# Counts of neighbours as 61-row products issued behind the lookups, with other costs and allowances in the slot planner

## The chip, the cores and the metric

The kernel runs on one core of one Trainium2 chip. The metric is the device time of one execution in microseconds (us); a comparison of two kernels is made on the same chip. The engines of the core work side by side, each on its own queue in order: TensorE (PE in the profile, its weight loads PEld), VectorE (DVE), ScalarE (ACT), GpSimd (POOL) and SyncE (SP, which issues transfers here).

## The reference

Four graph layers run over 16 graphs of 1024 nodes with 128 features, each followed by a layer norm over `x + layer(x)`. Cut to what matters:

```python
# layer 0: attention over the neighbours
h = clip(scores * mask, 0, CLAMP_HI) - NEG_PENALTY * (1 - mask);  out = softmax(h) @ v
# layer 1: a maximum over the neighbours
pre = p[:, :, None, :] + q[:, None, :, :] + b
out = max over neighbours j of relu(pre) * adj
# layer 2: a sum over the neighbours, then two dense products with a relu between
# layer 3: each graph's adjacency is first thinned row by row ("dilation", 1024 steps in order),
#          then three convolutions with batch norms, and a dense product
```

Layer 1 is `relu(p[i] + max of q[j] over the neighbours j of i)`, for each of 128 features.

## The kernel before, in words

**Subsets instead of neighbours.** The maximum of layer 1 is not taken neighbour by neighbour. The 1024 candidates of a graph are cut into groups of 6 (`GS`), and two groups make a subset step of 12 candidates (`PS`). For each group a table holds, for all 64 subsets of its 6 members, the maximum of q over that subset. For each node the subset that its adjacency row picks is looked up by a product: a 0/1 column ("hot") with one 1 among the 64 rows times the table. A graph has 86 such steps (`NP`), 16 graphs have 1376, and each step is a *slot* of two halves of 512 nodes. In a half:

- `count` (L799, L800) makes the hot columns for the slot after next: a product of the signs in `lit` with ten steps' worth of columns of the adjacency (`AT`, 120 rows, fp8) gives for each of the 128 (2 x 64) subsets how many of its members agree, and ACT's relu with the column `one_less` as bias leaves 1 where all do and 0 elsewhere.
- `look_up` (L830) does four products of 64 rows and 512 columns: the high part of the table for the two groups, then the low part, added up in PSUM (`pg`, two buffers of two banks).
- DVE takes the maximum of `pg` and the running `best` (L890), 128 x 1024 elements.

Every second slot, `table` (L811, L814) turns the next two steps' tables by TensorE and ACT copies out the high part; `low_part` (L819, L821) half a slot later subtracts the high part and copies the low part. The count's `pm` and the table's `pt` share two PSUM banks (tag `subset`).

**What runs between.** Everything else of layers 0, 1 and 2 (of the graph after and the graph before) and layer 3's dilation is cut into small pieces that a planner puts into the halves while the program is written. Streams written as generators (`scores`, `attend`, `rest`, `tables_of`) ask for an engine at a stated cost (`ask("PE", 0.86, ...)`). In each half each engine gets half of its allowance per slot (`ROOM`), at most one whole allowance saved up; a stream goes on while its engine's allowance is above zero, and the cost is taken off. The costs are microseconds of the author's; they decide only in which half a piece stands, not what it does. `dilation` has due times of its own, counted in slots; `dilate_on` emits its next part when it is due, and takes its DVE cost off. The pieces of PE share two PSUM banks by turns (tag `shared`, `taken` and `given`).

**The order in a half**, as the planner writes it, is the order of each engine's queue (`manual_schedule`): the lookup; the pieces; `low_part` in the first half of odd slots; `count` for the slot after next; `table` in the second half of even slots; the maximum. So on PE a count stands behind the pieces of its half, and on ACT its relu behind theirs.

**Loads.** `load_columns` (L744 to L751) brings `AT` for ten slots with one transfer on POOL's queue, two chunks ahead, into four buffers; a graph has nine chunks, the last of which has 64 rows and is cleared first (L750). The adjacency is float32 in memory and is converted by the transfer.

Ahead of the slots the first graph's scores are made, 132 us in all; behind them come layer 3's convolutions (from 5167 us on), which the change does not touch.

Of the kernel before, what the change touches and what calls it, by code (L numbers as in the profile page):

```python
# [43 lines left out]
PS = 2 * GS  # L44
PC = 10
CH = PC * PS
NP = -(-N // PS)
TG = 12
R, G = 32, 4
# [11 lines left out]
def subset_tables():  # L61

    half = P // 2
    s = np.arange(half)
    lit = np.zeros((CH, PC, P), np.float32)
    for j in range(CH):
        a, k = divmod(j % PS, GS)
        lit[j, j // PS, a * half:(a + 1) * half] = np.where((s >> k) & 1, 1.0, -1.0)
    size = sum((s >> k) & 1 for k in range(GS))
    return lit, np.tile(1.0 - size, 2).astype(np.float32).reshape(P, 1)  # L70


@with_exitstack
def tile_graph_layers(ctx: ExitStack, tc, a, out):
# [27 lines left out]
    nc.vector.memset(ones_b, 1.0)  # L102
    mhalf = consts.tile([P, T], F32, name="mhalf")
    nc.vector.memset(mhalf, -0.5)
    lit = consts.tile([CH, PC, P], F8, name="lit")
    nc.gpsimd.dma_start(out=lit, in_=a["lit"])
    less = consts.tile([P, P], F32R, name="less")
    nc.vector.tensor_scalar_mul(less, ident, -1.0)
    one_less = consts.tile([P, 1], F32, name="one_less")
    nc.sync.dma_start(out=one_less, in_=a["one_less"])  # L110

    def weight(name, shape=(P, P), how=None, pool=consts):
        t = pool.tile(list(shape), F32, name="w_" + name)
# [124 lines left out]
    def layers_012():  # L238
# [50 lines left out]

        def product_of(lhsT, rhs, dst, func, bias, delay=0.5):  # L290
            for h, s in enumerate(halves):
                yield ask("PE", 0.86, take=True, delay=0.5 if h else delay)
                p = shared("pp")
                nc.tensor.matmul(p, lhsT, rhs[:, s], start=True, stop=True)
                yield ask("A", 0.6, give=True, same=True)
                if bias is None:
                    nc.scalar.copy(dst[:, s], p)  # L297
                else:
                    nc.scalar.activation(dst[:, s], p, func, bias=bias)

        def scores(b):

            if b > 1:
                yield ask("Pool", 0, after=("p", b - 1))
            if b > 2:
                yield ask("Pool", 0, after=("rest", b - 3))
            load_rows(b)
            xT = w4.tile([P, N], F32, name="xT")
            yield from columns_of(xT, X[b])
            qT = w4.tile([P, N], F32, name="qT")  # L310
            yield from product_of(WqT, xT, qT, AF.Relu, bq)
            kT = w4.tile([P, N], F32, name="kT")
            yield from product_of(WkT, xT, kT, AF.Relu, bk)
            v = values[b] = w4.tile([P, T, D], F32, name="v")
            for h in range(2):
                yield ask("PE", 1.1, take=True)
                pv = shared("pv").rearrange("p (t d) -> p t d", d=D)
                nc.tensor.matmul(pv, ones_b[:3, :], four(bv3), start=True, stop=False)
                for t in range(4):
                    nc.tensor.matmul(pv[:, t, :], xT[:, (4 * h + t) * P:(4 * h + t + 1) * P], WvT,  # L320
                                     start=False, stop=(t == 3))
                yield ask("A", 0.6, give=True, same=True)
                nc.scalar.activation(v[:, 4 * h:4 * h + 4, :], pv, AF.Relu)
            for t in range(T):

                yield ask("A", 1.05)
                off = w4.tile([P, N], BF, name="off", tag="pen")
                nc.scalar.activation(off, An[b][:, t, :], AF.Identity, bias=ones[:, 0:1], scale=-1.0)
                if t > 1:
                    yield ask("PE", 0, same=True, after=("back", b, t - 2))  # L330
                e = w4.tile([P, N], F32, name="e", bufs=2)

                tops = small.tile([P, 2], F32, name="tops")
                for h, s in enumerate(halves):
                    yield ask("PE", 1.07, take=True)
                    psc = shared("psc")
                    nc.tensor.matmul(psc, qT[:, t * P:(t + 1) * P], kT[:, s], start=True, stop=False)
                    nc.tensor.matmul(psc, penalty, off[:, s], start=False, stop=True)
                    yield ask("V", 0.66, give=True)
                    nc.vector.tensor_scalar(e[:, s], psc, CLAMP_HI, None, op0=ALU.min, op1=ALU.max,  # L340
                                            accum_out=tops[:, h:h + 1])
                yield ask("V", 0.1, same=True)
                top = small.tile([P, 1], F32, name="top")
                nc.vector.tensor_scalar(top, tops[:, 0:1], tops[:, 1:2], -1.0, op0=ALU.max, op1=ALU.mult)
                yield ask("A", 1.1)
                total = small.tile([P, 1], F32, name="total")
                nc.scalar.activation(e, e, AF.Exp, bias=top, accum_out=total)
                exps[b, t] = e, total
                happened["e", b, t] = now
            yield ask("A", 0.01, after=("X1", b), delay=0.5)  # L350
            xT = w4.tile([P, N], F32, name="xT1", tag="xT")
            yield from columns_of(xT, X[b])
            q = w4.tile([P, NP * PS], F32, name="q", bufs=2)
            nc.gpsimd.memset(q[:, N:], LOWEST)
            yield from product_of(W01[:, 1, :], xT, q[:, :N], None, None)
            qs[b] = q
            happened["q", b] = now
            if b > 1:
                yield ask("A", 0, same=True, after=("y1", b - 2))
            p = ps[b] = w4.tile([P, N], F32, name="p", bufs=2)  # L360
            yield from product_of(Wd, xT, p, AF.Identity, b01)
            happened["p", b] = now

        def attend(b):
            for t in range(T):
# [14 lines left out]
                for h in range(2):  # L380
# [2 lines left out]
                        pav = shared("pav")[:, :D]  # L383
                    for c in range(4 * h, 4 * h + 4):
                        nc.tensor.matmul(pav, eT[:, c, :], values[b][:, c, :], start=(c == 0), stop=(c == T - 1))  # L385
                yield ask("V", 0.4, give=True)
                share = small.tile([P, 1], F32, name="share")
                nc.vector.reciprocal(share, total)
                nc.vector.scalar_tensor_tensor(y[:, t, :], pav, share, X[b][:, t, :], op0=ALU.mult, op1=ALU.add)
# [354 lines left out]
        def load_columns(at):  # L744
            b, c = divmod(at, T + 1)
            if b < B:
                rows = min(CH, N - c * CH)
                t = AT[at] = apool.tile([CH, N], F8, name="AT", bufs=4)
                if rows < CH:
                    nc.gpsimd.memset(t, 0.0)  # L750
                nc.gpsimd.dma_start(out=t[:rows], in_=adjT[b, c * CH:c * CH + rows])  # L751

        An, AT, subs, qs, ps, values, exps, bests, hots, tables = ({} for _ in range(10))
        now, taken, given, held = 0, 0, {}, {}
        pending = {}

        ROOM = {"PE": 1.2, "A": 0.8, "V": 2.2, "Pool": 9.0}
        room = dict.fromkeys(ROOM, 0.0)  # L760

        def start(stream, first=False):
# [29 lines left out]
        def count(s, h):  # L792
# [3 lines left out]
            if h == 0:  # L796
                hots[s] = w2.tile([P, N], F32R, name="hot", bufs=3)
            pm = psum.tile([P, 512], F32, tag="subset", name="pm", bufs=2)
            nc.tensor.matmul(pm, lit[:, r, :], AT[b * (T + 1) + c][:, halves[h]], start=True, stop=True)  # L799
            nc.scalar.activation(hots[s][:, halves[h]], pm, AF.Relu, bias=one_less)  # L800

        def table(s):

            b, g = divmod(s, NP)
            g0 = g - g % TG
            assert ("sub", b, g0) in happened, (s, [(x.__name__, pending[x]) for x in streams], room)
            pt = psum.tile([P, 512], F32, tag="subset", name="pt", bufs=2)[:, :2 * P]
            if g + 2 - g0 == min(TG, NP - g0):
                happened["used", b, g0] = now
# [5 lines left out]
            tables[s] = pt, high  # L815

        def low_part(s):
            pt, high = tables[s]
            nc.tensor.matmul(pt, less, high, start=False, stop=True, skip_group_check=True)  # L819
            low = w2.tile([P, 2 * P], F32R, name="low", bufs=2)  # L820
# [21 lines left out]
        def dilate_on():  # L842
            nonlocal due, wants_bank
            if due <= now and not (wants_bank and taken >= 2 and given.get(taken - 2, 1e9) > now):
                after, cost, wants_bank = next(dilate, (B * NP, 0, False))
                due += after
                room["V"] -= cost

        def slot(s, last):
# [11 lines left out]
                if b:  # L861
                    start(rest(b - 1))
            if s >= 0 and g % PC == 0:
                load_columns(b * (T + 1) + g // PC + 2)
            for h in range(2):
                now = s + 0.5 * h
                for e in ROOM:
# [1 line left out]
                if s >= 0:  # L869
                    pg = psum.tile([P, 2, 512], F32, tag="wide", name="pg", bufs=2)  # L870
                    look_up(s, h, pg)
                early = s >= 0 and due < now
                if early:
                    dilate_on()
# [3 lines left out]
                    dilate_on()  # L878
                if h == 0 and s % 2 and s + 1 < last:
                    low_part(s + 1)  # L880
                if s + 2 < last:
                    count(s + 2, h)
                    if h and s % 2 == 0:
                        table(s + 2)
                if s >= 0:
                    own = bests[b][:, :, halves[h]]
                    if g == 0:
# [6 lines left out]
        dilate = dilation()  # L894
        due, wants_bank = 0.0, False
        load_x(0)
        for at in range(2):
            load_columns(at)
        front, back = scores(0), attend(0)
        for t in range(T):  # L900
            while ("e", 0, t) not in happened:
# [332 lines left out]
```

## Time and profile before

| | us |
|---|---|
| median of 3 runs | 6459.39 (6446.67 to 6460.74) |
| the profiled execution | 6458.95 |
| its span, first to last instruction | 6457.2 |
| first lookup to last lookup | 132 to 5167 |
| mean granted TensorE clock | 0.93 of full |

In the profile a line such as `L890 DVE TENSOR_TENSOR best<-best,pg 128x1024 ... x2720 | 3258.7, 1215 | 556.8 <-PE pg L830 546.8` gives a group of equal instructions: their line, engine, operation, output and inputs, shape and number, then their busy time in us and the mean of one in ns, then how long the engine was idle just before them and what ended most of that. A line of the waits gives who waited for whom, the sum in us, how many times, and the longest. PE's ends are modelled: two products that follow each other are best compared by their starts. In the names, `128*128` or `64*128` is the part of the array that a product uses, rows first.

### The profile page before, as it was taken

To read this page: it belongs to the slowest core of one execution; us is meant where nothing else is said; L and a number is where in the kernel's file an instruction comes from. 1 tells how busy PE (TensorE), PEld (TensorE's weight loads), DVE (VectorE), ACT (ScalarE), POOL (GpSimd) and SP (SyncE) were. 2 spreads that over 40 slices of the span, in tenths; PEclk is the share of its full clock that TensorE was granted. 3 is DMA by queue.
4 is the path that set the end of the run, shared out by engine and by line. 5 is a ranking of instruction groups with operands and counts; after the bars stand their busy time and mean duration, and the time that the engine had idled before them with its cause. 6 is when DMAs were issued, how large, how long until landed. Compare 5 with 4: busy or idle time off the path is not lost. (4 is left out here: it accounts for less than half of the span.)

```text
span 6457.2 us, 90620 instructions
## 1 busy us (share of the span) xinstructions
PE 5729.3 (89%) x29184; PEld 2962.2 (46%) x29354; DVE 4978.8 (77%) x7877; ACT 3946.3 (61%) x7142; POOL 3502.1 (54%) x11319
## 2 busy tenths in 40 slices
PE   6989999989899999999989998989998867877998
PEld 3444444444444444444444444444443335555654
DVE  3888888888888888888888888888888834444445
ACT  4667666666667666766666666666665623333755
POOL 2665766666666666766666666666666511110113
PEclk8989899999899999999999999998998988888999
DMA  5121212121212121212121212121211065654545
GB/s 38 13 30 21 35 21 36 21 34 21 34 21 37 20 35 20 34 20 32 24 34 20 34 20 34 20 35 20 35 21 18 20 101 106 126 103 111 206 167 186
DMA packets 478402, 317.32 MB, mean 49 GB/s; under 512 B 301162, under 2 KB 429668, under 8 KB 473828
## 3 DMA queue, kind: packets, MB, share of 16 engines
q0 software_dynamic: 105648, 84.20, 15.0%
q1 hardware_dynamic: 367600, 226.13, 11.9%
q8 instruction: 230, 3.77, 0.2%
q10 hardware_dynamic: 4676, 1.19, 0.1%
q14 instruction: 248, 2.03, 0.1%
HBM read 412.71 MB, written 117.18 MB: 82 GB/s over the span
## 5 line engine op out<-in xcount | busy, mean ns | idle before, releaser
L890 DVE TENSOR_TENSOR best<-best,pg 128x1024 f32<-128x1024 f32 x2720 | 3258.7, 1215 | 556.8 <-PE pg L830 546.8
L800 ACT ACTIVATE hot<-pm,one_less 128x512 fp32r<-128x512 f32 x2752 | 1882.7, 689 | 736.9 <-PE pm L799 727.5
L830 PE MATMUL pg<-hot,high 64*128 64x512 f32 x5504 | 1436.1, 519 | 239.2 <-DVE best L890 231.4
L830 PE MATMUL pg<-hot,low 64*128 64x512 f32 x5504 | 1139.8, 411 | 0.0
L799 PE MATMUL pm<-AT,lit 120*128 120x512 fp8e4 x2752 | 1110.3, 404 | 20.9 <-ACT hot L800 8.5
L830 PEld LDWEIGHTS pg<-hot,high 64*128 64x128 f32 x5504 | 533.6, 191 | 1018.9 <-DVE best L890 510.5
L830 PEld LDWEIGHTS pg<-hot,low 64*128 64x128 f32 x5504 | 553.0, 198 | 0.0
L658 POOL TENSOR_SCALAR sc<-low_counts,half_mask,rest 16x1 f32<-16x1 f32 x992 | 351.8, 355 | 323.7 <-DVE rest L644 218.8
L799 PEld LDWEIGHTS <-lit 120*128 120x128 fp8e4 x2752 | 272.6, 99 | 520.5 <-issue 460.2
L663 POOL TENSOR_SCALAR sc<-sc 16x1 f32<-16x1 f32 x992 | 397.3, 401 | 105.1
L821 ACT CAST low<-pt 128x256 fp32r<-128x256 f32 x688 | 256.1, 372 | 258.2 <-PE pt L819 255.0
L1039 POOL TENSOR_TENSOR length<-length,mhalf 128x8 f32<-128x8 f32 x48 | 78.9, 1644 | 570.8 <-DVE length L1038 570.8
L660 POOL TENSOR_SCALAR sc<-sc 16x1 f32<-16x1 f32 x992 | 315.0, 318 | 107.7
L819 PE MATMUL pt<-high,less 128*128 128x256 f32 x688 | 294.1, 427 | 85.0 <-ACT high L814 78.2
L703 POOL TENSOR_SCALAR shifts<-centre 128x4 f32<-128x4 f32 x32 | 10.5, 327 | 656.9 <-DVE width L699 633.6
L665 POOL TENSOR_SCALAR hit<-V,sc 16x31 bf16<-16x31 bf16 (+30 forms) x992 | 361.1, 364 | 0.0
L666 POOL TENSOR_SCALAR last_rank<-V,sc 16x31 f32<-16x31 bf16 (+30 forms) x992 | 344.5, 347 | 0.0
L996 ACT CAST m<-near 128x1024 fp32r<-128x1024 fp8e4 x256 | 253.4, 1044 | 112.6 <-DVE near L965 59.6
L475 DVE TENSOR_TENSOR sub<-sub,q 128x24 f32<-128x24 f32 (+11 forms) x768 | 303.3, 396 | 24.0 <-ACT q L297 10.4
L811 PE MATMUL pt<-ident,sub 128*128 128x128 f32 x1376 | 286.1, 291 | 26.7 <-ACT hot L800 22.3
L385 PE MATMUL pav<-v,eT 128*128 128x128 f32 x2048 | 301.7, 293 | 2.1 <-ACT eT L378 2.1
L1009 PE MATMUL pagg<-m,high 128*128 128x512 f32 x768 | 277.3, 432 | 13.2 <-ACT high L1002 13.2
(268 smaller groups left out, 9754.6 us busy)
## 6 DMA issues: line engine op xcount, KB each, us to landing
removed<-gone SPq DMA_DIRECT2D x128, 256.0 KB
An<-in_adj_dram POOLq DMA_DIRECT2D x16, 1024.0 KB, 14.8
E<-in_adj_dram POOLq DMA_DIRECT2D x128, 128.0 KB, 5.8
gone_all<-removed POOLq DMA_DIRECT2D x64, 256.0 KB, 12.3
near<-in_adjT_dram POOLq DMA_DIRECT2D x16, 1024.0 KB, 17.9
kept<-near SPq DMA_DIRECT2D x16, 1024.0 KB
share<-share SPq DMA_DIRECT2D x32, 512.0 KB
hidden<-r SPq DMA_DIRECT2D x32, 512.0 KB
```

Of the source, the lines that this page charges most:

```text
L385: nc.tensor.matmul(pav, eT[:, c, :], values[b][:, c, :], start=(c == 0), stop=(c == T - 1))
L475: nc.vector.tensor_max(sub[:, :n_g, n:2 * n], sub[:, :n_g, 0:n], qg[:, 2 * g0:2 * g0 + n_g, k:k + 1].to_broadcast([P, n_g, n]))
L658: gp.tensor_scalar(half, mine, half_mask[:, m], rest[:, n:n + 1], op0=ALU.mult, op1=ALU.add)
L660: gp.tensor_scalar(sf, half, 5.5, sf, op0=ALU.is_gt, op1=ALU.mult)
L663: gp.tensor_scalar(to, at, sf, none, op0=ALU.subtract, op1=ALU.subtract)
L665: gp.tensor_scalar(hit[:, n, n + 1:], V[:, n, n + 1:], at, None, op0=ALU.is_equal)
L666: gp.tensor_scalar(last[:, n + 1:], V[:, n, n + 1:], to, None, op0=ALU.is_le)
L799: nc.tensor.matmul(pm, lit[:, r, :], AT[b * (T + 1) + c][:, halves[h]], start=True, stop=True)
L800: nc.scalar.activation(hots[s][:, halves[h]], pm, AF.Relu, bias=one_less)
L819: nc.tensor.matmul(pt, less, high, start=False, stop=True, skip_group_check=True)
L830: nc.tensor.matmul(pg[:, a], part[rows, at * P:(at + 1) * P], hots[s][rows, halves[h]], start=(k == 0), stop=(k == 1))
L890: nc.vector.tensor_max(own, own, pg)
```

## The change

1. The signs `lit` are stored twice, on partitions 0 to 59 and 64 to 123, for five steps each, in bf16; a 61st row holds one minus the size of each subset, and a row of ones in `AT` meets it. A count is then a product of 61 rows, on the lower or the upper half of the array, and its relu has no bias column.
2. `AT` is two fixed bf16 buffers, set to one at the start. A chunk is loaded as two transfers of 60 rows, one chunk ahead.
3. In a half, `count` stands right behind the lookup, ahead of the pieces.
4. Some asked costs are higher, the tables and the dilation's products are charged to PE's allowance, and the allowances per slot are 1.6 (1.2) for PE and 1.5 (2.2) for DVE.

What is computed stays the same.

```diff
+SUB = CH // 2
...
-    lit = np.zeros((CH, PC, P), np.float32)
-    for j in range(CH):
+    lit = np.zeros((2, half, PC // 2, P), np.float32)
+    for j in range(SUB):
         a, k = divmod(j % PS, GS)
-        lit[j, j // PS, a * half:(a + 1) * half] = np.where((s >> k) & 1, 1.0, -1.0)
+        lit[:, j, j // PS, a * half:(a + 1) * half] = np.where((s >> k) & 1, 1.0, -1.0)
...
-    lit = consts.tile([CH, PC, P], F8, name="lit")
+    lit = consts.tile([P, PC // 2, P], BF, name="lit")
     nc.gpsimd.dma_start(out=lit, in_=a["lit"])
+    for part in range(2):
+        nc.gpsimd.dma_start(out=lit[64 * part + SUB:64 * part + SUB + 1],
+                            in_=a["one_less"].rearrange("(o r) m -> o r m", o=1))
...
-                yield ask("PE", 0.86, take=True, delay=0.5 if h else delay)
+                yield ask("PE", 1.06, take=True, delay=0.5 if h else delay)
...
-                    yield ask("PE", 1.07, take=True)
+                    yield ask("PE", 1.24, take=True)
...
-                    yield ask("V", 0.66, give=True)
+                    yield ask("V", 0.77, give=True)
...
-                yield ask("V", 0.1, same=True)
+                yield ask("V", 0.21, same=True)
...
-                yield ask("V", 0.4, give=True)
+                yield ask("V", 0.51, give=True)
...
-                t = AT[at] = apool.tile([CH, N], F8, name="AT", bufs=4)
-                if rows < CH:
-                    nc.gpsimd.memset(t, 0.0)
-                nc.gpsimd.dma_start(out=t[:rows], in_=adjT[b, c * CH:c * CH + rows])
+                t = AT[at] = columns_in[at % len(columns_in)]
+                for part in range(-(-rows // SUB)):
+                    first = c * CH + part * SUB
+                    n = min(SUB, N - first)
+                    nc.gpsimd.dma_start(out=t[64 * part:64 * part + n], in_=adjT[b, first:first + n])
...
+        columns_in = [apool.tile([P, N], BF, name=f"AT{i}") for i in range(2)]
+        for t in columns_in:
+            nc.vector.memset(t, 1.0)
...
-        ROOM = {"PE": 1.2, "A": 0.8, "V": 2.2, "Pool": 9.0}
+        ROOM = {"PE": 1.6, "A": 0.8, "V": 1.5, "Pool": 9.0}
...
-            nc.tensor.matmul(pm, lit[:, r, :], AT[b * (T + 1) + c][:, halves[h]], start=True, stop=True)
-            nc.scalar.activation(hots[s][:, halves[h]], pm, AF.Relu, bias=one_less)
+            part, r = divmod(r, PC // 2)
+            rows = slice(64 * part, 64 * part + SUB + 1)
+            nc.tensor.matmul(pm, lit[rows, r, :], AT[b * (T + 1) + c][rows, halves[h]], start=True, stop=True)
+            nc.scalar.activation(hots[s][:, halves[h]], pm, AF.Relu)
...
         def table(s):
+            room["PE"] -= 0.22
...
         def low_part(s):
+            room["PE"] -= 0.23
...
         def dilate_on():
+                room["PE"] -= 0.4 * wants_bank
...
-                load_columns(b * (T + 1) + g // PC + 2)
+                load_columns(b * (T + 1) + g // PC + 1)
...
                     look_up(s, h, pg)
+                if s + 2 < last:
+                    count(s + 2, h)
                 early = s >= 0 and due < now
...
                     low_part(s + 1)
-                if s + 2 < last:
-                    count(s + 2, h)
-                    if h and s % 2 == 0:
-                        table(s + 2)
+                if h and s % 2 == 0 and s + 2 < last:
+                    table(s + 2)
```

## The prediction

> **What bounds the kernel now.** I read the page first, then the stretch that the change touches, then who waits for whom in it, then single instructions. The page's busy shares and costliest groups:
>
> ```profile
> PE 5729.3 (89%) x29184; PEld 2962.2 (46%) x29354; DVE 4978.8 (77%) x7877; ACT 3946.3 (61%) x7142; POOL 3502.1 (54%) x11319
> ...
> L890 DVE TENSOR_TENSOR best<-best,pg 128x1024 f32<-128x1024 f32 x2720 | 3258.7, 1215 | 556.8 <-PE pg L830 546.8
> ```
>
> The change lies in the slots, between the first lookup (L830, at 132 us) and the last (5167 us): 5035 us for 2752 half slots, 1.83 us each. The windows view of that stretch, with PE, PEld, DVE, ACT and POOL busy in this order:
>
> ```profile
> 132.00:5167.40 5035.40, 4599.42 (x24024) 2258.00 (x24189) 4364.95 (x6690) 3333.31 (x6297) 3267.28 (x10898) 0.94 0.19 26
> ```
>
> No engine is full: DVE works 4365 of 5035 us (87%). PE's ends are modelled, so I take PE by the distance between starts. The waits of the same stretch show why:
>
> ```profile
> ACT hot L800 <- PE pm L799: 727.5, 959, 5.2
> ...
> DVE best L890 <- PE pg L830: 546.8, 951, 7.7
> PEld pg L830 <- DVE best L890: 510.5, 920, 5.8
> PEld L799 <- issue: 459.6, 1250, 0.7
> PEld pg L830 <- issue: 411.5, 1478, 1.0
> ...
> ACT low L821 <- PE pt L819: 254.5, 359, 4.8
> PEld pt L819 <- ACT high L814: 238.4, 362, 12.3
> ```
>
> DVE waits for lookups 547 us and lookups wait for DVE 511 us: the two take turns, over two buffers of pg. 547 us is the most that a faster PE can give. The two "issue" rows belong to no semaphore; the timeline at full clock shows what they are:
>
> ```profile
> 2600.06 0.50 PE L830 MATMUL pg<-hot,high 64*128 64x512 f32 x2
> ...
> 2600.40 0.40 PE L830 MATMUL pg<-hot,low 64*128 64x512 f32 x2
> ...
> 2600.73 0.39 PE L799 MATMUL pm<-AT,lit 120*128 120x512 fp8e4 x1
> ...
> 2600.95 0.39 PE L811 MATMUL pt<-ident,sub 128*128 128x128 f32 x2
> ...
> 2603.39 0.40 PE L830 MATMUL pg<-hot,low 64*128 64x512 f32 x2
> ...
> 2603.72 0.39 PE L799 MATMUL pm<-AT,lit 120*128 120x512 fp8e4 x1
> ...
> 2604.04 0.50 PE L830 MATMUL pg<-hot,high 64*128 64x512 f32 x2
> ```
>
> A 512-column count is followed by a full-height product after 0.22 us (2600.73 to 2600.95), but by a 64-row lookup after 0.32 us, and a lookup's low half by a count after 0.33 us. Each passage between 64-row and full-height work costs 0.10 to 0.11 us.
>
> **The change part by part.** The order of instructions of both programs, cut at the lookups, gives the counts below.
>
> *Count behind the lookups, 61 rows.* Durations stay: 512 columns either way, ACT's relu 0.69 us with or without its bias column. What goes is passages. Where a half has no other PE work (607 halves before, 587 after) the round is 0.34 + 0.33 + 0.32 = 0.99 us; if all is 64-row work it is 3 x 0.22 = 0.66 us. Saved: 0.33 us, if lookups do not wait for DVE anyway. At full clock 545 such halves have a median of 0.99 us and a mean of 1.25: about half go at PE's pace. 587 x 0.33 x 0.5 = **97 us of PE time**. Where there are pieces, the passage out moves from ahead of the count to behind it: 0. Bounds: 0 (nothing saved) and 194 us (all of it).
>
> *low_part (L819).* It waits for ACT's high (317 us in all by its own line, 595 times), and without pieces starts 0.55 us after the low lookup. The count (0.22) now stands in that gap, and after L819 the lookup follows at some 0.31 us (its load 0.11, 256 columns 0.11, a passage 0.10) instead of 0.54 behind the count. 296 halves x 0.25 us, three quarters at PE's pace (the 75th percentile from L819 to the next lookup is 0.63 us, the median 0.55): **55 us**, at least 0, at most 94.
>
> *What the count now stands ahead of.* On PE it is ahead of the pieces, on ACT its relu is ahead of the pieces' copies, and pm and pt share two banks. The second count after low_part needs the bank that ACT's low copy frees. In the trace low ends 0.88 us (median; 0.77 at best, 1.18 at the 75th percentile) after L819 starts, and the next lookups' start plus 0.55 us left 0.30 us of room, because a count and a passage lay between. Those 0.32 us are gone and a relu of 0.69 us is now ahead of low. Behind that waiting count stand the half's pieces and the next lookup; best L890 of its own half is already fed. 395 of these 688 halves have pieces: 395 x 0.35 x 0.75 = 104 us if nothing covers it, 0 if DVE's own pieces do; I take **40**, since DVE is the fuller engine.
> Exp (L347) feeds the transposes L375 0.15 us (median) after it ends, so PE has no room there; behind a relu it ends some 0.9 us later relative to the lookups, of which the count ahead on PE covers 0.32: 128 x 0.55 = 70 us at most, 0 at least (ACT reaches exp late today as well); I take **30**. The other products have room: off to L338 1.8 us at the lower quartile, eT to L385 0.3, ET to L588 2.0.
>
> So PE gains 97 + 55 - 40 - 30 = 82 us. PE and DVE wait for each other about equally (511 and 547), so half arrives: **-41 us**.
>
> *Costs and allowances.* The same pieces are spread otherwise: 1168 halves without pieces instead of 1220; 22 instead of 31 runs of eight or more such halves. DVE's work of two neighbouring halves, from the groups' mean durations, has a 95th percentile of 4.98 us instead of 5.45. Taking in every half the larger of DVE's work and of 0.97 us plus PE's pieces, the sum over all halves is 4878 us for the old order and 4853 for the new: **-25 us**. Bounds: -50, and +25, as later pieces may pile up elsewhere.
>
> *AT columns.* Two DMAs of 60 rows for one of 120: 0.66 us more of POOL 144 times, POOL being at 65% there; the memsets of L750 (15 x 0.94 us) go. One chunk ahead instead of two: at a graph's end four slots remain, 12.2 to 19.1 us in the trace; POOL reached the load at most 3.7 us late there, and landing takes 3.8 us (median; worst 29.6). Hidden; uncovered, some 5 us, with the last graph's (POOL 22 us late once) 10. Two buffers also keep POOL from running ahead (it was up to 27 us ahead); it waits for DVE at shifts L703 633 us anyway. Setup has two more small DMAs on POOL and two memsets on DVE, one DMA less on SP: **+5**, 0 to 10.
>
> Sum: -41 - 25 + 5 = **-61 us**. The profiled execution took 6458.95 us, 1.75 over its span and 0.4 under the median: 6459 - 61 = **6398 us**.
>
> **The skill against the trace.** The Trainium skill, TensorEngine Tiling (Array Packing), Key Properties, has it that a change of tiling mode drains the engine; the 0.10 us passages are in line with it. Against the change stands TensorE: Matmul & The Clock Gate, Part 3: it says that a weight load overlaps running products only where the row group differs. By it the count's load could not hide behind the low lookup on its rows, 0.33 us would stay in one mode too, the 97 us would be nothing, and the sum some -12 us. The trace leans the other way without settling it: low's load is recorded 0.11 us after high's, while high is running.
>
> **The rivals.** *Stalls at the moved count (slower).* For: ACT's relu is already what follows PE most tightly (728 us of waiting), low and exp have no room. Against: ACT is at 66%. Price: 104 and 70 us in full, and the same kind of wait, 0.3 us, at high in the 392 low_part halves with pieces, 118: 292 against 152 saved, +140 on PE, of which half to all arrives, DVE's smoothing lost: 6530 to 6600. It decides from some 200 us of such waits, twice what I take.
> *DVE covers all.* PE's gain only lengthens its wait at L890, smoothing stays: 6439. For: the halves without pieces come in runs, where DVE is the bound.
> *No passage is saved* (the load cannot hide): term one gone, PE +15, so 6459 + 8 - 25 + 5 = 6447.
> *The clock.* 563 us of the stretch were at half clock, and these halves are longer by 128 us in all than the others of their kind. The page's PEclk row shows it; at 362 us it fell after 12 us with PE busy 72%. Less PE work could bring more of it, fewer piece-free runs less: 60 us either way, kept in the range.
>
> **How the numbers follow.** My case 0.50, stalls 0.27, DVE covers 0.13, no passage saved 0.10. A measurement here tells no change to 0.2%, 13 us. Faster is my case and most of DVE covers: 0.60; same, the no-passage case's middle: 0.10; slower, the stalls and the rest: 0.30. The range holds my case with all its terms arriving (-152 - 50 + 5 and more clock: 6310 leaves the tenth) and the stalls up to their middle: 6310 to 6530. Alone, my case runs from 6330 to 6440.
>
> **What would show it.** Right: low to count and count to lookup 0.22 us; the two issue rows under 600 us together; DVE best waiting for pg under 480 us. Wrong: counts waiting for ACT's low or hot above 100 us, or L375's loads waiting for exp above 100 (51 now); PE's wait for DVE growing by as much as the issue rows lose; more than 650 us at half clock.

## The result, and the profile after

The changed kernel takes **6500.9 us** (median of 7 runs, 6476.44 to 6514.92) against 6459.5 for the kernel before, a ratio of 1.0065 with a 95% interval of 1.0047 to 1.0083. It is slower by 0.65%; 6398 us were forecast.

The profiled execution is the fastest of the seven: 6476.44 us, with a span of 6474.6 and a mean granted TensorE clock of 0.905 (before: 6457.2 and 0.934). So the trace explains the smaller part of the difference, some 18 us of 41; the mean clock of the other six executions was 0.899 to 0.903, and they are the slower ones. What follows compares profiled executions, with times at half clock that are of one execution each; the verdicts go by the medians.

The page of the changed kernel: busy time by engine, the granted clock in 40 equal slices (tenths of full speed), and the two costliest groups.

```profile
PE 5785.5 (89%) x29185; PEld 3100.1 (48%) x29354; DVE 4963.5 (77%) x7879; ACT 3786.6 (58%) x7142; POOL 3578.6 (55%) x11449
...
PEclk8999898989997989999999898899897778888999
...
L901 DVE TENSOR_TENSOR best<-best,pg 128x1024 f32<-128x1024 f32 x2720 | 3263.0, 1215 | 577.9 <-PE pg L840 566.0
L808 ACT ACTIVATE hot<-pm 128x512 fp32r<-128x512 f32 x2752 | 1644.2, 598 | 1421.6 <-PE pm L807 1397.9
```

The same row of the page of before, which the prediction mentioned and did not show:

```profile
PEclk8989899999899999999999999998998988888999
```

The reader should see that PE is busier by 56 us although it does the same number of products with the same columns (29185 against 29184), that ACT is freer, and that the clock row has 7s and 8s where before it had 9s. The stretch of the slots, in the windows view (length, then PE, PEld, DVE, ACT and POOL busy, clock, DMA share, GB/s):

```profile
128.50:5183.10 5054.60, 4652.51 (x24025) 2394.51 (x24189) 4347.87 (x6692) 3173.77 (x6297) 3342.65 (x11026) 0.91 0.19 30
```

It is 5054.6 us long instead of 5035.4: this stretch holds the whole difference of the profiled executions. PE has 53 us more to do in it, DVE 17 us less, and the clock fell from 0.94 to 0.91. By the clock's own records 926 us of it ran at half clock, in 81 pieces, instead of 563 us in 66.

The waits in that stretch (who waited for whom, sum in us, times, longest):

```profile
ACT hot L808 <- PE pm L807: 1396.4, 2031, 4.7
PEld L807 <- issue: 763.8, 2486, 0.5
DVE best L901 <- PE pg L840: 565.7, 808, 3.3
...
PEld pg L840 <- DVE best L901: 510.8, 835, 4.2
...
PEld pg L840 <- issue: 213.7, 814, 1.5
POOL AT L754 <- PE pm L807: 132.4, 36, 18.4
...
PEld pt L829 <- ACT high L823: 74.1, 161, 1.7
...
PEld pe L377 <- ACT e L349: 68.3, 81, 2.1
...
PE pe L377 <- ACT e L349: 43.1, 65, 1.8
...
PE pt L829 <- ACT high L823: 27.1, 49, 1.4
PEld pg L840 <- ACT low L831: 21.1, 39, 1.2
...
PE pm L807 <- ACT hot L808: 4.3, 12, 0.6
```

Three rows of the kernel before, in the same view:

```profile
PE pt L819 <- ACT high L814: 77.7, 231, 11.9
PEld pe L375 <- ACT e L347: 50.7, 76, 1.5
PE pe L375 <- ACT e L347: 18.6, 29, 1.0
```

These rows are taken up point by point below. In short: what the change was to take out of PE's way did go (`low_part`, now L829, waits 74.1 + 27.1 = 101 us for ACT's high instead of 238.4 + 77.7 = 316), the stalls that I feared at the moved count are not there (4.3 us at L807), and DVE nevertheless waits longer for lookups, 566 us instead of 547. ACT waits far longer for counts (1396 us instead of 728), where its relu now is the first thing behind each lookup; ACT is busy 63% of the stretch, and this row costs nothing by itself.

What happened instead shows in the timeline of PE (start, duration, line, tiles, form, number; the last column is the idle time before):

```profile
2605.10 0.39 PE L807 MATMUL pm<-AT,lit 61*128 61x512 bf16 x1
2606.49 0.50 PE L840 MATMUL pg<-hot,high 64*128 64x512 f32 x2 [1.00 <-DVE best L901]
2606.83 0.39 PE L840 MATMUL pg<-hot,low 64*128 64x512 f32 x2
2607.07 0.39 PE L807 MATMUL pm<-AT,lit 61*128 61x512 bf16 x1
2607.72 0.50 PE L840 MATMUL pg<-hot,high 64*128 64x512 f32 x2 [0.27 <-DVE best L901]
2608.06 0.48 PE L840 MATMUL pg<-hot,low 64*128 64x512 f32 x2
2608.33 0.65 PE L807 MATMUL pm<-AT,lit 61*128 61x512 bf16 x1
2608.91 0.69 PE L820 MATMUL pt<-ident,sub 128*128 128x128 f32 x2
2609.53 0.80 PE L840 MATMUL pg<-hot,high 64*128 64x512 f32 x2
2610.12 0.63 PE L840 MATMUL pg<-hot,low 64*128 64x512 f32 x2
2610.55 0.65 PE L807 MATMUL pm<-AT,lit 61*128 61x512 bf16 x1
```

The passage that was forecast to go has gone: the low half of a lookup and the count behind it start 0.24 us apart (2606.83 to 2607.07), where it was 0.33. Then, behind halves that held nothing but lookups and 61-row counts, with PE idle for 1.00 us ahead of one of them, the clock falls at 2608.2: the same count now lasts 0.65 us instead of 0.39, the lookup's high half 0.80 instead of 0.50.

### The profile page after: what moved, and what is told of

It is laid out like the page before. It is cut to its first block, busy times and chain, and to the rows that moved or that the text cites. A ratio compares the mean times of both kernels' runs of the same rounds, so it can differ in the third digit from the quotient of the medians.

```text
span 6474.6 us, 90787 instructions
## 1 busy us (share of the span) xinstructions
PE 5785.5 (89%) x29185; PEld 3100.1 (48%) x29354; DVE 4963.5 (77%) x7879; ACT 3786.6 (58%) x7142; POOL 3578.6 (55%) x11449
## 5 line engine op out<-in xcount | busy, mean ns | idle before, releaser
L808 ACT ACTIVATE hot<-pm 128x512 fp32r<-128x512 f32 x2752 | 1644.2, 598 | 1421.6 <-PE pm L807 1397.9
L840 PE MATMUL pg<-hot,high 64*128 64x512 f32 x5504 | 1529.7, 538 | 273.9 <-DVE best L901 255.5
L840 PE MATMUL pg<-hot,low 64*128 64x512 f32 x5504 | 1245.7, 427 | 8.4 <-ACT low L831 8.3
L807 PE MATMUL pm<-AT,lit 61*128 61x512 bf16 x2752 | 1164.7, 423 | 5.1 <-ACT hot L808 4.3
L840 PEld LDWEIGHTS pg<-hot,high 64*128 64x128 f32 x5504 | 605.0, 199 | 903.7 <-DVE best L901 510.8
L807 PEld LDWEIGHTS <-lit 61*128 61x128 bf16 x2752 | 277.4, 101 | 776.3 <-issue 764.7
L840 PEld LDWEIGHTS pg<-hot,low 64*128 64x128 f32 x5504 | 623.4, 206 | 33.2 <-ACT low L831 21.1
L823 ACT CAST high<-pt 128x256 fp32r<-128x256 f32 x688 | 255.2, 371 | 122.1 <-PE pt L820 120.6
L829 PE MATMUL pt<-high,less 128*128 128x256 f32 x688 | 298.4, 434 | 27.3 <-ACT high L823 27.1
L820 PE MATMUL pt<-ident,sub 128*128 128x128 f32 x1376 | 302.8, 305 | 4.8 <-ACT hot L808 1.6
```

The source lines that it names most:

```text
L807: nc.tensor.matmul(pm, lit[rows, r, :], AT[b * (T + 1) + c][rows, halves[h]], start=True, stop=True)
L808: nc.scalar.activation(hots[s][:, halves[h]], pm, AF.Relu)
L840: nc.tensor.matmul(pg[:, a], part[rows, at * P:(at + 1) * P], hots[s][rows, halves[h]], start=(k == 0), stop=(k == 1))
```

## The experiments

The three things that the change does can be done one by one: the **rows** (61-row counts with their loads and the relu without bias), the **order** (the count right behind the lookup) and the **costs** (the asked costs, charges and allowances). All eight combinations were run, the kernel before and the changed one among them. Each ratio is to the kernel before, measured beside the run. In the expectations "theory C" is that of the clock: less array work behind the lookups lets the clock fall more often, and that costs more than the saved passages bring. Its rivals look for the loss in waits that the moved order makes, or in the other costs.

How the time at half clock is read: the trace records when the granted clock changes. Its sum over the stretch of the slots is given for each run.

**e1: the rows alone**, at the old place and costs.

```diff
-            nc.tensor.matmul(pm, lit[:, r, :], AT[b * (T + 1) + c][:, halves[h]], start=True, stop=True)
-            nc.scalar.activation(hots[s][:, halves[h]], pm, AF.Relu, bias=one_less)
+            part, r = divmod(r, PC // 2)
+            rows = slice(64 * part, 64 * part + SUB + 1)
+            nc.tensor.matmul(pm, lit[rows, r, :], AT[b * (T + 1) + c][rows, halves[h]], start=True, stop=True)
+            nc.scalar.activation(hots[s][:, halves[h]], pm, AF.Relu)
...
+        columns_in = [apool.tile([P, N], BF, name=f"AT{i}") for i in range(2)]
```

> The kernel before with the 61-row counts alone: at the old place behind the pieces, with the old costs and allowances. Theory C (clock): the gate of TensorE's clock weighs rows, so 61-row counts alone bring most of the time at half clock: 750 us or more in the slots instead of 563, and the time is no better than before, 6460 to 6510 us, although the passages of piece-free halves are gone as well. Rival S (stalls of the moved count and relu): half clock stays near 560 us and the time falls to 6400 to 6440, because the passages go and nothing has moved. Rival P (costs and allowances): as S.

Measured: 6398.9 us, ratio 0.9909 (0.9894 to 0.9924); 778 us at half clock; stretch 4979.2 us. The time at half clock rose by 215 us as the clock theory has it, but the kernel got faster, which I had not expected: what the rows save at the old place pays for it. The time is that of the rivals, the half clock that of theory C, so this run alone decides nothing.

**e2: the rows undone**, order and costs as changed.

```diff
-            part, r = divmod(r, PC // 2)
-            rows = slice(64 * part, 64 * part + SUB + 1)
-            nc.tensor.matmul(pm, lit[rows, r, :], AT[b * (T + 1) + c][rows, halves[h]], start=True, stop=True)
-            nc.scalar.activation(hots[s][:, halves[h]], pm, AF.Relu)
+            nc.tensor.matmul(pm, lit[:, r, :], AT[b * (T + 1) + c][:, halves[h]], start=True, stop=True)
+            nc.scalar.activation(hots[s][:, halves[h]], pm, AF.Relu, bias=one_less)
```

> The changed kernel with the old 120-row counts, their bias column and their loads, but at the new place behind the lookups and with the new costs. Theory C: half clock back to 560 us give or take 80, and 6430 to 6470 us. Rival S: the order is the changed one and the passages are back, so 6500 us or more with half clock near that of before. Rival P: half clock stays near 900 us, time 6500 or more.

Measured: 6362.9 us, ratio 0.9863 (0.9848 to 0.9879); 379 us at half clock. Better than expected, and both rivals (6500 us or more) fall. Order and costs together are worth 1.4%, and the rows edit, put on top of them, costs 2.0% (e8 below parts the 61 rows from the rest of that edit). The windows view of its stretch, for comparison with the one above:

```profile
130.50:5069.20 4938.70, 4464.00 (x24025) 2239.00 (x24189) 4335.52 (x6691) 3364.55 (x6296) 3305.43 (x10898) 0.96 0.19 27
```

The same 24025 products take PE 4464 us here and 4653 us in the changed kernel; the clock is 0.96 against 0.91.

**e3: the costs undone**, rows and order as changed.

```diff
-        ROOM = {"PE": 1.6, "A": 0.8, "V": 1.5, "Pool": 9.0}
+        ROOM = {"PE": 1.2, "A": 0.8, "V": 2.2, "Pool": 9.0}
...
-            room["PE"] -= 0.22
...
-            room["PE"] -= 0.23
...
-                room["PE"] -= 0.4 * wants_bank
```

> The changed kernel with the old costs and allowances of the planner. Theory C: half clock stays at 800 us or more and the time at 6490 or more (25 us of smoothing lost). Rival P: half clock near 560 us and the time at or under 6460. Rival S: as slow as the changed kernel, half clock unchanged.

Measured: 6531.2 us, ratio 1.0114 (1.0096 to 1.0132); 1111 us at half clock. The costs are not where the loss comes from: without them it is larger.

**e7: the order alone; e4: the costs alone; e5: the order undone.** They complete the eight.

```diff
                     look_up(s, h, pg)
+                if s + 2 < last:
+                    count(s + 2, h)
...
-                if s + 2 < last:
-                    count(s + 2, h)
-                    if h and s % 2 == 0:
-                        table(s + 2)
+                if h and s % 2 == 0 and s + 2 < last:
+                    table(s + 2)
```

> The kernel before with the counts behind the lookups alone: old 120-row counts, old costs. Theory C: half clock 560 or less, and 6385 to 6430 us, as low_part finds ACT's high ready and nothing lowers the clock. Rival S (the moved count and relu stall PE): 6470 us or more.

> The kernel before with the new costs and allowances alone. My prediction's term: 25 us less, 6420 to 6445 us, half clock about 560. If the spread of pieces matters more than that through the clock, half clock below 480 and 6400 or less.

> The changed kernel with the counts back behind the pieces: 61 rows and new costs remain. Theory C by rows alone says as with the rows alone, 6375 to 6400 us, with half clock at 700 to 800 us. If it is the new costs that do not get along with 61 rows, it stays above 6450 and half clock at 850 or more.

Measured: e7 6387.2 us, ratio 0.9895 (0.9881 to 0.991); e4 6398.8, 0.9915 (0.9902 to 0.9928); e5 6405.2, 0.9928 (0.9915 to 0.9942). e7 came as theory C had it. e4 came as the second case of its expectation, in which the spread of the pieces works through the clock. e5 has the half clock that was expected and is 5 us slower than its range. With that the table is full (median in us, and in brackets the us at half clock within the slots):

| order, costs | 120 rows | 61 rows |
|---|---|---|
| old, old | 6459.5 (563) | 6398.9 (778) e1 |
| old, new | 6398.8 (372) e4 | 6405.2 (748) e5 |
| new, old | 6387.2 (515) e7 | 6531.2 (1111) e3 |
| new, new | 6362.9 (379) e2 | 6500.9 (926) the change |

Each of the three parts makes the kernel before faster by about 1% when it is done alone. The 61 rows add 215 to 596 us at half clock in every line; at the old place this is paid for (about so with the new costs), in the new order it is not.

The two columns of each line have the same pieces in the same halves, so they can be compared half by half. A half is taken from one lookup's start to the next, and sorted by whether the clock was at half for more than 2% of it. Sum of the differences in us, with the number of halves in brackets, for the step from the first kernel to the second:

| step | all | full in both | full, then half | half, then full | half in both |
|---|---|---|---|---|---|
| before to e1 | -56 | -84 (2290) | +89 (190) | -36 (55) | -25 (216) |
| e4 to e5 | +7 | -80 (2330) | +108 (244) | -25 (27) | +3 (150) |
| e7 to e3 | +145 | -11 (2187) | +178 (304) | -10 (18) | -12 (242) |
| e2 to the change | +115 | -14 (2259) | +169 (310) | -19 (30) | -21 (152) |
| e8 (below) to the change | +156 | +4 (2270) | +174 (311) | -10 (19) | -12 (151) |

The 310 halves that lose the full clock between e2 and the changed kernel are somewhat shorter than the others (1.67 us in the mean against 1.73) and become 2.22 us. They alone cost 169 us. Where the clock is full in both, the 61 rows bring 80 to 84 us in the old order and only 11 to 14 us in the new one.

**e6: what the clock looks at.** To the end of the kernel before, work is added that nothing uses: streams of 512-column bf16 products on different parts of the array, each behind a pause in which PE has nothing to do; then four streams with no pause between them.

```diff
+    def stream(n, *parts):
+        banks = [bank("gate") for _ in parts]
+        for _ in range(n):
+            for p, (lo, hi) in zip(banks, parts):
+                nc.tensor.matmul(p, gw[lo:hi], gx[lo:hi], start=True, stop=True)
+
+    for parts in (((0, 128),), ((0, 120),), ((0, 96),), ((0, 61),), ((0, 64), (64, 128)), ((0, 61), (64, 125))):
+        pause()
+        stream(100, *parts)
+    pause()
+    stream(100, (0, 128))
+    stream(100, (0, 61))
+    stream(100, (0, 128))
+    stream(100, (0, 32))
```

> The kernel before with a test of the clock appended: seven streams of 512-column bf16 products with 128, 120, 96 and 61 rows, with 64+64 and 61+61 rows on both halves of the array, each behind a pause; then, without pauses, 128, 61, 128 and 32 rows, 100 rounds each. Theory C (the gate weighs rows): 128, 120 and 64+64 rows bring the clock up within 4 to 8 us, 61 rows alone stay at half clock for all of their 43 us, 96 rows stand on the edge; behind a full-clock stream 61 rows keep the clock and 32 rows lose it within 7 us. If the gate weighs busy time and not rows, all streams come up within 4 to 8 us and none falls. Span some 300 to 500 us longer.

One execution was taken. The windows view of these products alone (length, busy time of PE and number of products, granted clock, DMA share, GB/s). In order: 128 rows; 120; 96; three windows of the 61 rows alone, whose stream lasts from 6535.4 to 6578.2; 64 rows beside 64; 61 beside 61; then, without a pause, 128, 61, 128, and 32 rows in two windows. The windows with a clock of 1.00 are laid behind the rise, which came 2.8 to 4.5 us after a stream's start (3.6 for 96 rows, 3.1 for 61 beside 61). The first stream is left out of these figures, since it began while the kernel's last work still ran.

```profile
6440.00:6454.00 14.00, 13.89 (x65) 1.00 0.22 63
6472.00:6488.00 16.00, 16.00 (x76) 1.00 0.00 1
6506.00:6523.00 17.00, 17.00 (x81) 1.00 0.00 0
6536.00:6550.00 14.00, 14.00 (x34) 0.50 0.00 1
6550.00:6564.00 14.00, 14.00 (x35) 0.50 0.00 0
6564.00:6578.00 14.00, 14.00 (x34) 0.50 0.00 0
6595.00:6612.00 17.00, 17.00 (x160) 1.00 0.01 1
6630.00:6647.00 17.00, 17.00 (x162) 1.00 0.00 1
6668.00:6681.00 13.00, 12.95 (x61) 1.00 0.00 0
6682.00:6703.00 21.00, 21.00 (x99) 1.00 0.00 1
6704.00:6724.00 20.00, 19.95 (x94) 1.00 0.00 1
6726.00:6733.00 7.00, 7.00 (x26) 0.76 0.00 0
6733.00:6760.00 27.00, 27.00 (x64) 0.50 0.00 0
```

PE is busy all the time in all of them (13.89 of 14 us at the least), and yet 61 rows alone stay at half clock for 43 us, 96 rows do not, and two streams of 61 rows side by side do not either. Behind a stream at full clock, 61 rows keep it (21 us in the window) and 32 rows lose it. So the clock goes by time weighted with rows in use, and what brings full clock back (between 61 and 96 of 128 rows at 100% busy) is more than what keeps it (between 32 and 61). Whether it counts single rows or blocks of them, and whether columns count too, no run tells.

The slots agree as to the falls. All stretches at one clock in these traces are whole multiples of 3.41 us. I took the 3.41 us ahead of each change of the clock and added up the time in which products streamed, from their columns, each times its share of the 128 rows. Ahead of a fall this share was at most 0.37 to 0.39 in nine of ten cases, in the kernel before, the changed one and the variants alike; unweighted the same bound was 0.38 before and 0.46 in the changed kernel, so the unweighted share is not what decides. Ahead of a return the weighted share was 0.71 or more in nine of ten cases (median 0.78 to 0.83), but of the windows that stay at half clock in the changed kernel (median 0.69) one in ten has over 0.78 too: for the return this sum draws no sharp line. The four products of a lookup run two by two on both halves of the array (their starts are 0.003 us apart); a 61-row count weighs half of what a 120-row count weighs: it gives 0.09 of the windows that stay at half clock, in the mean, where counts gave 0.14 before. Against e2, with the same pieces in the same halves, the changed kernel falls to half clock more often (81 times against 59) and stays there longer (11.4 us in the mean against 6.4). That the lighter counts keep the work just under what brings the clock back fits this; it is argued, not shown by itself.

**e8: the changed kernel with the count over the whole height.** Only the rows of the product change: 125 rows, with zeros in `lit` for the half that isn't meant, and fp8 for `lit` instead of bf16. Columns, loads, order, costs and the relu without bias stay; the passages between 64-row and full-height work come back.

```diff
-    lit = np.zeros((2, half, PC // 2, P), np.float32)
+    lit = np.zeros((2, half, 2, PC // 2, P), np.float32)
...
-    lit = consts.tile([P, PC // 2, P], BF, name="lit")
+    lit = consts.tile([P, PC, P], F8, name="lit")
...
-            part, r = divmod(r, PC // 2)
-            rows = slice(64 * part, 64 * part + SUB + 1)
+            rows = slice(0, 64 + SUB + 1)
```

> The changed kernel with one thing other: a count runs over rows 0 to 124 at once, the signs of the other half being zeros (held as fp8 to fit), so it is a full-height product in the same place, with the same sums, loads, relu, costs and order. It brings the passages back. Theory C (the gate weighs rows): half clock falls from 926 us to 380 give or take 100, and the time to 6340 to 6400 us, though PE has more passages to make. Rival L (the bf16 buffers, the loads in two parts or one chunk ahead make it slow): half clock stays above 800, and 6480 us or more.

Measured: **6319.7 us, ratio 0.9796 (0.9782 to 0.981)**, somewhat better than expected; 335 us at half clock. Rival L falls. The stretch in the windows view, and three rows of the waits within it:

```profile
130.10:5027.90 4897.80, 4432.33 (x24025) 2225.76 (x24189) 4328.38 (x6691) 3142.20 (x6297) 3339.71 (x11025) 0.97 0.19 31
```

```profile
PEld L807 <- issue: 1030.8, 2746, 0.7
PEld pg L840 <- DVE best L901: 561.0, 941, 4.1
DVE best L901 <- PE pg L840: 438.1, 676, 9.5
```

Of DVE's wait for lookups 438 us are left, of 566. The last line of the table of halves says how e8 and the changed kernel differ: at full clock not at all (4 us over 2270 halves), and by 174 us in the 311 halves that only the changed kernel runs at half clock. Nothing but the rows (and the weights' type) of one product differs between the two. This is the fastest version of all that were run. Against e2 (120 rows, with bias column and the old loads) its stretch is 41 us shorter, so the rest of the rows edit is a gain, and the 61 rows themselves cost 2.7% by the two ratios (1.0065 against 0.9796).

**f3: the changed kernel with work that is useless but for the clock.** In 541 halves that have no pieces of PE, behind the count, two full-height products whose result nothing reads.

```diff
+                spent = room["PE"], taken
...
+                if s >= 0 and spent == (room["PE"], taken) and given.get(taken - 2, 1e9) <= now:
+                    p = shared("fill")
+                    given[hold()] = now
+                    for _ in range(2):
+                        nc.tensor.matmul(p, ident_b, upto, start=True, stop=True)
```

> The changed kernel with work that nothing uses: in each of 541 halves without any other PE work, two full-height 512-column products into a free shared bank, behind the count (0.43 us and two passages, 0.63 us a half, 340 us of PE time in all). Theory C (low row-weighted activity costs the clock): half clock falls from 926 to 600 us or less, and the kernel gets faster by its useless work, 6400 to 6480 us against 6501. If the clock is not what costs the time, PE's extra work makes it slower: 6560 us or more.

Measured: 6470.9 us, ratio 1.0019 to the kernel before (1.0008 to 1.0029), so 0.5% faster than the changed kernel; 399 us at half clock instead of 926.

```profile
127.20:5172.60 5045.40, 4776.15 (x25271) 2308.17 (x25271) 4370.99 (x6692) 3175.16 (x6297) 3345.29 (x11023) 0.96 0.19 30
```

PE does 1082 products more (two in 541 halves) and the stretch is 9 us shorter. Half by half: 315 halves get the full clock back and save 158 us, while the halves at full clock in both pay 106 us for the useless products.

**f1 and f2: e8 with one or two such products** in the same halves (the same diff, with `range(1)` in f1).

> The changed kernel with full-height counts, and one such product in each of the same halves. Theory C: half clock from 335 to 200 us or less; the time 6270 to 6320, if the 0.21 us per half are covered by DVE; 6330 to 6360 if they are not.

> As the run before with two such products. Theory C: half clock 100 us or less; 6260 to 6340 us, with the product's own time the larger part of what is left.

Measured: 6336.2 us, ratio 0.9812 (0.9796 to 0.9829), and 6380.8, 0.9882 (0.9865 to 0.9899); 266 and 246 us at half clock. Both miss: more remains at half clock than I had expected (200 us or less, and 100 or less), f2 is slower than its range, and on top of e8 the fill costs more than it gains. What the remaining 250 us come from was not followed up.

## Why the prediction was wrong, point by point

**The passages (97 us of PE time).** Right in size, wrong in what arrives. At full clock the halves without other PE work went from 1.21 to 1.03 us between e2 and the changed kernel, 452 halves, -81 us. But the halves with pieces, which I costed at nothing because the passage only moves behind the count, went from 1.861 to 1.898 us, 1807 halves, +67 us. Of the 81 us 14 remain. What takes the 67 us shows in the starts. In the halves with pieces the count follows the lookup 0.09 us sooner and the first piece follows the count 0.09 us later (medians), so the passage did move, as forecast. But where the first pieces are f32 products of full height, the second of them is late as well: in `psc` (the scores) it starts 0.533 us after the one ahead of it instead of 0.433 (183 pairs), in `pav` (the attention's sums) 0.213 instead of 0.113. The kernel before has the same 0.533 and 0.213 where such pieces follow a lookup directly. So a passage to f32 pieces costs some 0.2 us, twice what I had, and it was e2 that avoided the second half of it, by a full-height count in between. PE's idle time ahead of the next lookup did not grow in these halves (0.06 us in the mean both times), so it is not DVE that takes the 67 us. In the halves without pieces that idle time grew from 0.25 to 0.31 us: the rival that DVE covers holds there for a part. The mark for my case, DVE waiting less than 480 us for lookups, was missed at 566; e8, with passages but more full clock, has 438.

**The rival that no passage is saved** fell. The Trainium skill, TensorE: Matmul & The Clock Gate, Part 3, has a weight load overlap only with products of another row group. Here low and count use the same rows and follow each other after 0.24 us instead of 0.33, so its load doesn't stand in the way. It is the two "issue" rows that I misread: together they are 978 us, more than before (871) instead of under 600, and in e8, where the passages are back, 1030.8 at the count alone. They don't measure passages; the spacing of starts does, and I had both. What they do measure is left open.

**low_part (55 us).** Right in sign: its waits for ACT's high in the slots fell from 316 us to 74.1 + 27.1 = 101. That is more than was forecast for that place; how much of it arrived, no run shows by itself. Nor is the order its only cause: with the rows alone (e1) the same waits are 165.7 + 28.4 = 194 us, with order and costs (e2) 106.3 + 51.1 = 157.

**The waits at the moved count (40 us), and the rival of stalls.** Too high. Counts waited for ACT's hot 4.3 us, lookups for ACT's low 21.1 + 8.3. The whole order, with 120 rows, made the stretch 73 us shorter (5035.4 to 4962.6 us, e7). The wait at exp is the one that came as said: 68.3 + 43.1 = 111 us at L377 in the slots instead of 69 for L375 before, +42 where I had +30; the loads' own share, 68.3 us, stayed under my mark of 100.

**Costs and allowances (-25 us).** Alone (e4) they made the stretch 60 us shorter, and the median 0.85%. The time at half clock fell from 563 to 372 us with it: charging the halves evenly also leaves fewer halves without array work, which fits the gain; no run tests it by itself. The sum of the prediction had nothing for it.

**AT and the relu.** POOL waited 132 us for counts to release a buffer at L754, and no lookup or count waited for a load: hidden, as said. The relu takes 598 ns instead of 689, which I had put as unchanged (0.69 us "with or without its bias column"); in e2, with the bias column, it is 689 ns again.

**The clock is the step that failed.** The prediction had it as "60 us either way, kept in the range", with less PE work as a possible cause of more half clock, and gave it no chance of its own. It reckoned PE work as time and didn't see that a 61-row product, of the same duration, weighs half as much. Its own mark, "more than 650 us at half clock", was passed with 926. In the sum it stood at nothing; measured, half clock went from 563 to 926 us, and the 311 halves that the changed kernel alone runs at half clock, against e8 with full-height counts, cost 174 us. e8, which takes the same time where both run at full clock (4 us over 2270 halves), is 2.0% faster than the kernel before. How near the rest of the sum was can't be read off: order and costs with 120 rows (e2) came to 6363 us, but with 184 us less at half clock than before, which the sum did not have either. The rows edit then cost 115 us of the stretch (2.0% by the two ratios), where I had it as a gain. As for the range, the sum given for its lower end, -152 - 50 + 5, comes to 6262 us, and to 6322 with 60 us of clock; 6310 is a choice between them.

**The order and the rows work against each other.** At the old place the 61-row count stood directly ahead of the next lookup in 1487 of the halves of e1 that had full clock in both, and in 1057 of them the lookup started within 0.05 us of the count's start: one of its two high products uses the other rows (the one recorded second starts 0.04 us later and lasts 0.58 us instead of 0.50; the trace does not tell which of the two it is). In the kernel before, the step from count to lookup there took 0.32 us. In the changed kernel 54 of 319 halves at full clock have such a start; behind the lookup, with pieces following or DVE not ready, the rest is lost. The gain at the old place sits in the halves with `low_part`, where the count stands between it and the lookup: 577 halves, -169 us from before to e1, but 568 halves, +7 us, from e2 to the changed kernel. The shorter relu may have a part in it, as `low_part` also starts 0.21 us sooner in e1 (mean of 230 such halves without other pieces). This is read from the traces; that it is the whole of the difference between 80 and 14 us was not tested.

## What to carry to other kernels

Before a product is cut to fewer rows, look at how often the clock falls around it: here a 61-row product that ran alone took as long as one of full height (0.39 us) and counted about half for the clock, so that padding it with zero rows was faster than the smaller form. Read the granted clock per stretch in every comparison, and compare half by half at equal clock, since a mean over both clocks mixes two effects of opposite sign. Where three edits come together, try them in all combinations: here each alone gained about 1%, and two of them together, rows and order, lost 1.1%.

## What the hardware showed that was not expected

- **The clock weighs rows.** 61-row products back to back, with PE busy for 100% of 43 us, never reached full clock; 96 rows, or two 61-row streams beside each other, did after 3.6 and 3.1 us. Rows that hold zeros count too: e8's padded counts bring half clock from 926 to 335 us. The Trainium skill, TensorE: Matmul & The Clock Gate, Part 1, says that the gate judges how busy PE was over a window of 3413 ns and knows half and full clock. The two levels (0.50 and 1.00, the 0.76 above being a window with one change in it) agree; "busy" has to be read as rows in use times time.
- **It holds more easily than it rises.** 61 rows kept full clock for 21 us behind a 128-row stream, and 32 rows lost it; in the slots nine of ten falls came at a weighted share of 0.39 or less, and nine of ten returns at 0.71 or more.
- **A bias column costs ACT time.** 689 ns with it, 598 without, for a relu of 128 x 512 out of PSUM.
- **A 61-row product hardly holds up a pair of 64-row products on both halves of the array.** In e1, where a 61-row count is the last product ahead of a lookup, the lookup's first product started 0.004 us (median) after it, both 512 columns wide.
- **A passage to f32 products shows twice.** Behind 64-row or 61-row work the first full-height f32 product is some 0.10 us late, and the second is 0.10 us late once more (`psc` 0.533 us after the first instead of 0.433, `pav` 0.213 instead of 0.113).
